# Order of the key and value projections in a four-layer Perceiver kernel, and the number of projection pieces issued per stage

## The chip, the core and the metric

The kernel runs as one program on one core of a Trainium2 chip. The metric is device time in microseconds (us) of one execution; the time of a kernel is the median of its runs. Engines are named as the profile names them: PE is TensorE (PEld its weight loads), DVE is VectorE, ACT is ScalarE, POOL is GpSimd, SP is SyncE. DMA transfers are issued by SP, ACT and POOL and carried out by 16 DMA engines.

## What is computed

The state x has 128 rows of 256 numbers. Four layers follow each other, and each has a cross attention over a context of 12,544 rows of 256 numbers, a self attention and a feed-forward part:

```python
x = x + L0_xattn(layernorm(x), ctx, mask, ...)     # l0x
x = x + L0_attn(layernorm(x), ...)                 # l0a
x = x + L0_ffn(layernorm(x), ...)                  # l0f: 16 experts
x = x + L1_xattn(ctx, ctx, layernorm(x), fside_SxS2, fside_BxS2, ...)   # l1x
x = x + L1_attn(layernorm(x), ...)                 # l1a
x = x + L1_ffn(layernorm(x), ...)                  # l1f: 8 experts
x = x + L2_xattn(layernorm(x), ctx, ctx, ...)      # l2x
x = x + L2_attn(layernorm(x), ...)                 # l2a
x = x + L2_ffn(layernorm(x), ...)                  # l2f: piecewise linear GELU
x = x + L3_xattn(layernorm(x), ctx, ctx, mask, ...)   # l3x
x = x + L3_attn(layernorm(x), ...)                 # l3a
x = x + L3_ffn(layernorm(x), ...)                  # l3f: 8 experts
```

A cross attention has 16 heads of 16 numbers:

```python
q = split_heads(x @ Wq + bq)
k = split_heads(ctx @ Wk + bk)      # 12,544 keys
v = split_heads(ctx @ Wv + bv)
logits = einsum('bhqd,bhkd->bhqk', q, k) / 4 + mask terms
out = einsum('bhqk,bhkd->bhqd', softmax(logits), v)
```

l1x also adds a 128 x 12,544 table to the logits. All data is 32-bit. The keys and values of all four layers depend on the context alone, and on nothing that an earlier layer computes.

## The kernel before

**Projection pieces.** `projections` (line 181) makes for each layer a list of jobs, here called pieces, and appends all four lists to one queue, `self.jobs`. The context is cut into 25 chunks c of 512 rows (the last has 256). A piece does one of four things with one chunk: "K" projects the first eight heads' keys, "k" the other eight heads' keys, "V" and "W" the values of the chunk's first and second 256 rows. A layer has 99 pieces. The string of a *pass* gives the order: with `"KkVW"`, each chunk's four pieces follow each other, chunk by chunk; `["KVW", "k"]` goes through all chunks with K, V, W and then through all chunks again with k. Each pass loads every chunk once.

- A key piece (`keys`, line 224) is one PSUM bank of PE work (128x512, two contraction halves). ACT copies the result with its bias into the first half of a staging tile "kst", DVE writes the rounding remainder into its second half (line 231), and two DMAs of 256 KB, issued by POOL (line 236), write the halves to DRAM. "kst" has two buffers.
- A value piece (`values`, line 245) is one bank of PE work, and ACT copies it into a staging tile `vst`, of which there are two. After the second of a chunk (or the only one of the last) POOL issues one DMA of 544 KB (line 265).
- The chunk itself, 512 KB, is loaded by SP (line 216) into one of three buffers. The first piece of each chunk in a pass asks for the loads of this chunk and the next two (of the first two only, for the first piece of a layer). The layer's projection weights are loaded by POOL (line 211) along with its first chunk; each layer's `load` knows only its own chunks.

**When pieces run.** Pieces are taken from the front of the queue in three ways. `pump(n)` takes n. `need(keys)` takes pieces until the named ones are done. And outside the cross attentions every call of `one` (a PSUM bank for a step of l0a, l0f, ...) first takes one piece, so that a piece stands between two steps of these stages on PE; l2f also pumps once for each of its 16 kinks (line 1218).

**A cross attention** (`cross`, line 383) goes through *ticks* in an order written out by hand; PE, ACT, DVE, POOL and SP each follow the order in which the program issues to them. A tick covers up to 2048 keys in four strips of 512 for one head. In tick n, PE computes the scores of tick n, and DVE takes their maximum per query ("first"). `lag` ticks later the scores are computed again, transposed and with the maximum subtracted ("second"), ACT takes the exponential, and PE multiplies with the values. l0x, l2x and l3x have 104 ticks and a lag of 15; l1x works on groups of four heads and has 100 ticks and a lag of 27. So the first `lag` ticks have only score work, the last `lag` only the second half. At tick n SP is told to load the key tiles of tick n+2 (`load_first`, 256 KB) and the value tiles of the second part two ticks ahead (`load_second`). Before the key tiles of a block of 2048 keys are loaded, `need` makes sure that the K or k pieces of this block and the next are done; for the values, the same with V and W.

**Numbers of pieces.** At each tick `cross` pumps as many pieces as `counts` (line 1410) says for its layer. By these rules and the passes, 100 pieces run up to the end of l0x (all 99 of l0x, one of l1x), 57 in l0a and l0f, 121 in l1x, 69 in l1a and l1f, 15 in l2x, 29 in l2a and l2f, 5 in l3x.

**Other tiles** named below: `l0x_c`, `l1x_c`, ... are context chunks; `l1x_ks` is l1x's staged key tile and `l1x_kx` its place in DRAM; `vst` and `l1x_vx` the same for values; `l1x_kw` are key projection weights; `l0x_s`, `l0x_t` are the first and second scores (and `l0x_s<-l0x_kx` the key tile's load); `l1x_f`, `l1x_g` are tiles of l1x's added table.

Of the kernel before, what the change touches and what calls it, by code (L numbers as in the profile page):

```python
# [70 lines left out]
def _block(b):  # L71

    return (4, SEG) if b < NB - 1 else (2, P)
# [8 lines left out]
def r32(ap):  # L82

    return ap.bitcast(F32R)
# [10 lines left out]
class Net:  # L95
# [84 lines left out]

    def projections(self, names):
        self.kx, self.vx = {}, {}
        for l, name in enumerate(CROSS):
            if name not in names:
                continue
            gw = 17 * GROUP[name]
            for b in range(NB):
                ns, seg = _block(b)
                self.kx[name, b] = self.dp.tile([16, 32 * ns, seg], F32, name=f"{name}_kx{b}",
                                                tag=f"{name}_kx{b}")  # L190
                self.vx[name, b] = self.dp.tile([272 // gw, P, ns * seg // P, gw], F32,
                                                name=f"{name}_vx{b}", tag=f"{name}_vx{b}")
            if l == 0:
                passes = ["KVW", "k"]
            else:
                passes = ["KkVW"]
            self.project(name, passes)

    def project(self, name, passes):

        nc = self.nc
        order = [(p, c) for p in passes for c in range(NCH)]
        ctx, held = {}, {}

        def load(n):
            if n >= len(order) or n in ctx:
                return
            if n == 0:
                for kv, half in (("k", 0), ("v", 512)):
                    w = self.bp.tile([P, 512], F32, name=f"{name}_{kv}w", tag=f"{kv}w")  # L210
                    nc.gpsimd.dma_start(out=w, in_=self.io[f"w_{name}_kv"][:, half : half + 512])
                    held[kv] = w.rearrange("p (c f) -> p c f", c=2)
            c = order[n][1]
            m = min(SEG, S2 - c * SEG)
            t = self.bp.tile([P, 2, SEG], F32, name=f"{name}_c{n}", tag="ctx", bufs=3)
            nc.sync.dma_start(out=t[:, :, :m],
                              in_=self.io["ctxT"][:, c * SEG : c * SEG + m]
                              .rearrange("(c p) k -> p c k", p=P))
            ctx[n] = t

        def keys(n, half, c):
            m = min(SEG, S2 - c * SEG)
            b, t = c // 4, c % 4
            ns, seg = _block(b)
            k = self.bp.tile([P, 2, SEG], F32, name=f"{name}_ks{half}_{c}", tag="kst")
            ps = self.bank(f"{name}_k{half}_{c}")
            self.mm(ps[:, :m], [held["k"][:, i, half * P : (half + 1) * P] for i in range(2)],
                    [ctx[n][:, i, :m] for i in range(2)])
            kb = self.col(f"{name}_kb")[:, half : half + 1]
            nc.scalar.activation(r32(k[:, 0, :m]), ps[:, :m], AF.Identity, bias=kb)  # L230
            nc.vector.scalar_tensor_tensor(out=r32(k[:, 1, :m]), in0=ps[:, :m], scalar=kb,
                                           in1=k[:, 0, :m], op0=ALU.add, op1=ALU.subtract)
            for at in range(0, m, seg):
                r = 32 * (t + at // seg)
                for i in range(2):
                    nc.gpsimd.dma_start(
                        out=self.kx[name, b][8 * half : 8 * half + 8,
                                             r + 16 * i : r + 16 * i + 16, :],
                        in_=k[:, i, at : at + seg])

        def values(n, part, c):
            G = GROUP[name]
            b = c // 4
            if part == 0:
                held["vs"] = self.vst[self.nvst % 2]
                self.nvst += 1
            v = held["vs"].rearrange("p (g h) a e -> p g a h e", h=G)
            vf = held["vs"].rearrange("p h a e -> p (h a e)").rearrange(
                "p (g a h e) -> p g (a h) e", g=16 // G, a=4, h=G)
            ps = self.bank(f"{name}_v{c}_{part}")  # L250
            for i in range(2):
                at = (2 * part + i) * P
                self.mm(ps.rearrange("p (g i f) -> p g i f", g=16 // G, i=2)[:, :, i, :],
                        [ctx[n][:, j, at : at + P] for j in range(2)],
                        [held["v"][:, j, :].rearrange("p (g f) -> p g f", g=16 // G)
                         for j in range(2)])
            nc.scalar.copy(vf[:, :, 2 * part * G : (2 * part + 2) * G, 0:16],
                           ps.rearrange("p (g j e) -> p g j e", g=16 // G, e=16))
            last = c == NCH - 1
            if part == 1 or last:  # L260
                m = 2 if last else 4
                flat = held["vs"].rearrange("p h a e -> p (h a e)").rearrange(
                    "p (g f) -> p g f", g=16 // G)
                at = 4 * (c % 4)
                nc.gpsimd.dma_start(
                    out=self.vx[name, b][:, :, at : at + m, :].rearrange("g p a e -> p g (a e)"),
                    in_=flat[:, :, : m * 17 * G])

        for n, (parts, c) in enumerate(order):
            for kind in parts:  # L270
                if kind == "W" and c == NCH - 1:
                    continue

                def job(n=n, c=c, kind=kind, first=kind == parts[0]):
                    if first:
                        for i in range(3 if n else 2):
                            load(n + i)
                    if kind in "Kk":
                        keys(n, int(kind == "k"), c)
                    else:  # L280
                        values(n, int(kind == "W"), c)
                self.jobs.append(((name, kind, c), job))
# [100 lines left out]
    def cross(self, name, side=False, project=True, quota=None):  # L383
# [6 lines left out]
        with ExitStack() as es:  # L390
# [307 lines left out]
            lag = per + LEAD  # L698
            pending = None
            load_queries(0)  # L700
            with tc.manual_schedule():
                qs[0] = queries(0)
                for n in range(len(ticks) + lag):
                    load_first(n + 2)
                    if n >= lag - 2:
                        load_second(n - lag + 2)
                    new = scores(n if n < len(ticks) else None, n - lag if n >= lag else None)
                    if n < len(ticks) and n % per == per - 1:
                        lower(n // per)
                    if n >= per and n % per == 0 and n // per <= 16 // G:  # L710
                        spread(n // per - 1)
                    if n % per == per // 3 and n // per + 1 < 16 // G:
                        load_queries(n // per + 1)
                    if n % per == 2 * per // 3 and n // per + 1 < 16 // G:
                        qs[n // per + 1] = queries(n // per + 1)
                    self.pump(quota(n, len(ticks), lag))
                    if n >= lag:
                        if pending:
                            values(pending)
                        if n > lag + 1 and (n - lag - 1) % per == 0:  # L720
                            finish((n - lag - 1) // per - 1)
                        pending = new
                values(pending)
                finish(16 // G - 1)
# [457 lines left out]
    def l2_ffn(self):  # L1182

        nc = self.nc
        with self.tc.tile_pool(name="l2f", bufs=1) as pool, \
# [27 lines left out]
            for i, (at, c) in enumerate(_gelu_kinks()):  # L1213
                t = a
                if i:
                    t = rp.tile([P, 1024], F32, name=f"l2f_k{i}", tag="k")
                    nc.scalar.activation(t, a, AF.Relu, bias=self.const("kinks")[:, i : i + 1])
                self.pump(1)
                nc.vector.scalar_tensor_tensor(out=y, in0=t, scalar=c, in1=y, op0=ALU.mult,
                                               op1=ALU.add)  # L1220
            nc.vector.tensor_scalar(out=h, in0=h, scalar1=0.0, scalar2=None, op0=ALU.max)
# [178 lines left out]
    def run(self, steps):  # L1400
# [4 lines left out]
        for i in range(8):  # L1405
# [2 lines left out]
        self.masks(names)  # L1408
        self.projections(names)
        counts = {  # L1410
            "l0x": lambda n, m, lag: int(n % 3 > 0) if 14 <= n < 54 else 0,
            "l1x": lambda n, m, lag: int(n % 4 != 3),
            "l2x": lambda n, m, lag: int(n < lag),
            "l3x": lambda n, m, lag: int(n < lag),
        }
# [196 lines left out]
```

## Time and profile before

| | us |
|---|---|
| median of 3 runs | 2657.65 (2648.64 to 2659.61) |
| the profiled execution | 2661.88 |
| its span, first to last instruction | 2660.1 |

| stage, by the timeline | from | to | us |
|---|---|---|---|
| start to l0x's first maximum | 0 | 96 | 96 |
| l0x, from the first maximum to the last exponential | 96 | 586 | 490 |
| l0a, l0f, start of l1x | 586 | 773 | 187 |
| l1x, ticks 0 to 26 (scores only) | 773 | 942 | 169 |
| l1x, rest | 942 | 1470 | 528 |
| l1a, l1f, start of l2x | 1470 | 1721 | 251 |
| l2x | 1721 | 2085 | 364 |
| l2a, l2f, start of l3x | 2085 | 2195 | 110 |
| l3x | 2195 | 2553 | 358 |
| l3a, l3f | 2553 | 2660 | 107 |

Within l0x, the first maximum of tick 8 is at 185, of tick 22 at 236, of tick 27 at 259, of tick 53 at 380 and of tick 54 at 394.

The page's first part gives the share of the span in which each engine was busy; the second part cuts the span into 40 slices of 66.5 us and shows tenths:

```profile
PE 2412.7 (91%) x41075; PEld 1874.3 (70%) x41075; DVE 1719.1 (65%) x3814; ACT 1229.3 (46%) x2256; POOL 419.6 (16%) x803
...
PE   7789989999968799999999898799999949999969
...
PEclk9889999999978889989899999899999967999979
DMA  8887774418967798877778676674343563444315
```

PE is busy for 91% of the span. The slices in which it is not (the first two, 12 to 14, 25, 32) are the start, the beginning of l1x, l1f and l2f. In the instructions' views a line gives start, duration, engine, line of the kernel, operation, tiles (what is written `<-` what is read), shapes, and in brackets how long the engine had been idle before it and what ended that wait.

### The profile page before, as it was taken

The page shows a single profiled execution, that of the slowest core. Times are in us where ns is not written, and L with a number is a line of the kernel's source. Part 1 is how long each engine was busy: PE and PEld are TensorE (multiplying, and loading weights), DVE is VectorE, ACT ScalarE, POOL GpSimd, SP SyncE. Part 2 cuts the span into 40 slices and gives each one's busy share as a digit, 9 for nine tenths or more (in the row PEclk, how much of TensorE's full clock was granted, in tenths as well). Part 3 has the DMA queues.
Part 4 walks back from the last instruction along what each step waited for, and adds up shares of the span by engine and source line. Part 5 has one row for each costly group of instructions (what it writes and reads, how often), then busy time and mean ns, then how long its engine had stood idle before and what let it go on. Part 6 is the DMA issues. An engine that isn't in the chain of part 4 may idle for free. (4 is left out here: it accounts for less than half of the span.)

```text
span 2660.1 us, 94232 instructions
## 1 busy us (share of the span) xinstructions
PE 2412.7 (91%) x41075; PEld 1874.3 (70%) x41075; DVE 1719.1 (65%) x3814; ACT 1229.3 (46%) x2256; POOL 419.6 (16%) x803
## 2 busy tenths in 40 slices
PE   7789989999968799999999898799999949999969
PEld 5567668886745577677677665478888737888858
DVE  1247668834134599989887753398887358888731
ACT  2225546663312145444457334446666532666642
POOL 3321110003322311111111332210000221000001
PEclk9889999999978889989899999899999967999979
DMA  8887774418967798877778676674343563444315
GB/s 277 246 260 216 226 215 135 134 53 287 296 195 215 232 323 276 298 251 256 274 246 274 188 205 196 198 238 137 115 137 95 155 193 100 136 119 135 102 49 208
DMA packets 256707, 524.56 MB, mean 197 GB/s; under 512 B 55692, under 2 KB 71510, under 8 KB 252326
## 3 DMA queue, kind: packets, MB, share of 16 engines
q1 hardware_dynamic: 175488, 309.75, 35.1%
q0 software_dynamic: 79312, 206.56, 26.6%
q8 instruction: 323, 5.29, 0.8%
q10 hardware_dynamic: 1494, 2.23, 0.2%
q14 instruction: 90, 0.74, 0.1%
HBM read 360.41 MB, written 157.79 MB: 195 GB/s over the span
## 5 line engine op out<-in xcount | busy, mean ns | idle before, releaser
L585 ACT ACTIVATE l1x_e<-l1x_e 128x512 f32<-128x512 f32 x392 | 234.0, 632 | 243.8 <-DVE l1x_e L579 243.8
L562 DVE CUSTOM_DVE_ANT_0 l1x_j<-l1x_s,l1x_f 128x512 f32<-128x512 f32 (+1 forms) x416 | 254.3, 655 | 55.3 <-DMA l1x_f<-in_fside 28.6
L567 DVE TENSOR_REDUCE l3x_mxs<-l3x_s 128x1 f32<-128x512 f32 (+1 forms) x400 | 244.1, 673 | 58.3 <-PE l3x_s L613 58.2
L567 DVE TENSOR_REDUCE l2x_mxs<-l2x_s 128x1 f32<-128x512 f32 (+1 forms) x400 | 249.2, 675 | 43.1 <-PE l2x_s L613 37.3
L567 DVE TENSOR_REDUCE l0x_mxs<-l0x_s 128x1 f32<-128x512 f32 (+1 forms) x400 | 244.3, 673 | 49.4 <-PE l0x_s L613 49.1
L585 ACT ACTIVATE l0x_e<-l0x_t 128x512 f32<-128x512 f32 (+1 forms) x400 | 203.9, 593 | 127.5 <-PE l0x_t L613 122.7
L585 ACT ACTIVATE l3x_e<-l3x_t 128x512 f32<-128x512 f32 (+1 forms) x400 | 203.8, 593 | 114.0 <-PE l3x_t L613 110.2
L585 ACT ACTIVATE l2x_e<-l2x_t 128x512 f32<-128x512 f32 (+1 forms) x400 | 203.5, 594 | 112.9 <-PE l2x_t L613 112.9
L579 DVE TENSOR_TENSOR l1x_e<-l1x_t,l1x_g 128x512 f32<-128x512 f32 x392 | 243.3, 683 | 11.2 <-PE l1x_t L613 10.0
L613 PE MATMUL l1x_t<-l1x_q,l1x_t 32*128 32x128 f32 x3136 | 174.0, 268 | 3.9 <-DMA l1x_t<-l1x_kx 3.6
L613 PE MATMUL l3x_t<-l3x_q,l3x_s 32*128 32x128 f32 x3136 | 171.3, 260 | 0.0
L613 PE MATMUL l0x_t<-l0x_q,l0x_s 32*128 32x128 f32 x3136 | 168.5, 259 | 3.0 <-issue 3.0
L613 PE MATMUL l2x_t<-l2x_q,l2x_s 32*128 32x128 f32 x3136 | 165.2, 262 | 0.0
L613 PEld LDWEIGHTS l3x_t<-l3x_q,l3x_s 32*128 32x128 f32 x3136 | 164.0, 189 | 0.0
L613 PE MATMUL l1x_s<-l1x_mrow,l1x_cq 32*128 32x256 f32 (+1 forms) x800 | 136.1, 333 | 30.1 <-DVE l1x_mxs L562 14.7
L613 PEld LDWEIGHTS l0x_t<-l0x_q,l0x_s 32*128 32x128 f32 x3136 | 161.0, 186 | 3.3 <-issue 3.3
L613 PEld LDWEIGHTS l1x_t<-l1x_q,l1x_t 32*128 32x128 f32 x3136 | 157.5, 190 | 6.9 <-DMA l1x_t<-l1x_kx 6.8
L613 PE MATMUL l1x_s<-l1x_s,l1x_q 32*128 32x256 f32 (+1 forms) x1600 | 150.8, 298 | 6.1 <-DMA l1x_s<-l1x_kx 5.9
L613 PE MATMUL l0x_s<-l0x_s,l0x_q 32*128 32x256 f32 (+1 forms) x1600 | 149.9, 289 | 6.2 <-DMA l0x_s<-l0x_kx 6.2
L613 PE MATMUL l2x_s<-l2x_s,l2x_q 32*128 32x256 f32 (+1 forms) x1600 | 150.4, 308 | 3.8 <-DMA l2x_s<-l2x_kx 3.5
L613 PEld LDWEIGHTS l2x_t<-l2x_q,l2x_s 32*128 32x128 f32 x3136 | 153.5, 186 | 0.0
L613 PE MATMUL l3x_s<-l3x_s,l3x_q 32*128 32x256 f32 (+1 forms) x1600 | 152.1, 289 | 0.2 <-issue 0.2
(668 smaller groups left out, 5788.0 us busy)
## 6 DMA issues: line engine op xcount, KB each, us to landing
l0x_c<-in_ctxT SPq DMA_DIRECT2D x48, 512.0 KB
l0x_kx<-l0x_ks POOLq DMA_DIRECT2D x96, 256.0 KB, 7.8
l0x_s<-l0x_kx SPq DMA_DIRECT2D x96, 256.0 KB
l1x_kx<-l1x_ks POOLq DMA_DIRECT2D x96, 256.0 KB, 6.7
l1x_s<-l1x_kx SPq DMA_DIRECT2D x96, 256.0 KB
l1x_f<-in_fside SPq DMA_DIRECT2D x96, 256.0 KB
l2x_kx<-l2x_ks POOLq DMA_DIRECT2D x96, 256.0 KB, 6.2
l1x_t<-l1x_kx SPq DMA_DIRECT2D x96, 256.0 KB
```

Source lines behind the costliest of these rows:

```text
L562: nc.vector.tensor_tensor_reduce(out=junk[:, :seg], in0=bank[:, j * seg : (j + 1) * seg], in1=ft[g, b][t][:, :seg], scale=1.0, scalar=-3.0e38,
L567: nc.vector.tensor_reduce(out=out, in_=bank[:, : len(hs) * seg].rearrange("p (h k) -> p h k", h=len(hs)), axis=AX.X, op=ALU.max)
L579: nc.vector.tensor_tensor(out=e[:, t, :m].rearrange("p (h q) -> p h q", h=G), in0=src.rearrange("p (h q) -> p h q", h=G), in1=ft["t", g, b ...
L585: nc.scalar.activation(e[:, t, :m], src, AF.Exp)
L613: nc.tensor.matmul(out, lhs, rhs, start=start, stop=stop, skip_group_check=True)
```

## The change

The queue's order and the numbers of pieces change; what each piece does does not.

- l0x's passes become "K" and then "VWk": the first eight heads' keys of all chunks come first, then chunk by chunk the values and the other keys. l1x and l3x get two passes, "Kk" and "VW": all keys, then all values, with each chunk loaded twice. l2x stays with "KkVW".
- The loads of all layers form one list, `self.loads`, and the first piece of a chunk issues loads up to two further on in this list, also across the end of a layer.
- In `cross`, the loads for the second part are issued ahead of those for the first part of the same tick.
- l2f pumps at every third kink, six times instead of 16.
- `counts` has other numbers for l0x and l1x.

With this, 114 pieces run up to the end of l0x (its own 99 by tick 21, and 15 keys of l1x in ticks 22 to 26), 57 in l0a and l0f (35 keys, then 22 value pieces), 123 in l1x (40 in ticks 0 to 26, where there were 46), 69 in l1a and l1f (3 of l2x, then all 50 keys of l3x, then 16 value pieces), 15 in l2x, 18 in l2a and l2f, none in l3x.

```diff
     def projections(self, names):
         self.kx, self.vx = {}, {}
+        self.loads, self.fetched = [], 0
...
             if l == 0:
-                passes = ["KVW", "k"]
+                passes = ["K", "VWk"]
             else:
-                passes = ["KkVW"]
+                passes = ["KkVW"] if name == "l2x" else ["Kk", "VW"]
             self.project(name, passes)
...
         ctx, held = {}, {}
+        base = len(self.loads)
 
         def load(n):
-            if n >= len(order) or n in ctx:
-                return
             if n == 0:
...
         for n, (parts, c) in enumerate(order):
+            self.loads.append(lambda n=n: load(n))
             for kind in parts:
...
                     if first:
-                        for i in range(3 if n else 2):
-                            load(n + i)
+                        while self.fetched < min(len(self.loads), base + n + 3):
+                            self.loads[self.fetched]()
+                            self.fetched += 1
...
                 for n in range(len(ticks) + lag):
-                    load_first(n + 2)
                     if n >= lag - 2:
                         load_second(n - lag + 2)
+                    load_first(n + 2)
...
-                self.pump(1)
+                if i % 3 == 0:
+                    self.pump(1)
...
-            "l0x": lambda n, m, lag: int(n % 3 > 0) if 14 <= n < 54 else 0,
-            "l1x": lambda n, m, lag: int(n % 4 != 3),
+            "l0x": lambda n, m, lag: 0 if n < 10 else 2 if n < lag else 3 if n < 27 else 0,
+            "l1x": lambda n, m, lag: 1 + n % 2 if n < lag else int(n % 6 > 0),
             "l2x": lambda n, m, lag: int(n < lag),
             "l3x": lambda n, m, lag: int(n < lag),
```

## The prediction

> **What bounds the kernel now.** I read the engines' busy time over stretches first, then the timelines of PE and ACT, then the DMA issues. "Piece" is one pump job: a key piece (K; k for the second half) or half a value pair (V, W).
>
> ```profile
> 32.00:82.00 50.00, 45.61 (x165) 31.64 (x163) 5.75 (x8) 13.14 (x23) 17.60 (x26) 0.97 0.97 280
> 642.00:740.00 98.00, 92.57 (x430) 70.08 (x429) 19.71 (x36) 31.24 (x56) 34.66 (x55) 0.97 0.93 313
> 821.00:890.00 69.00, 57.79 (x312) 37.65 (x311) 23.62 (x58) 15.35 (x25) 20.78 (x33) 0.89 0.80 235
> 1505.00:1575.00 70.00, 69.89 (x373) 52.91 (x372) 52.35 (x137) 24.18 (x40) 26.06 (x40) 1.00 0.73 206
> ```
>
> Columns: stretch, us, busy PE, PEld, DVE, ACT, POOL, granted PE clock, DMA share, GB/s. PE is nearly full everywhere, but at the start and in l0f the DMA engines are full too (0.97, 0.93).
>
> ```profile
> 21.43 1.88 PE L343 MATMUL l0x_k<-l0x_c,l0x_kw 128*128 128x512 f32 x4
> 23.15 3.62 PE L343 MATMUL l0x_v<-l0x_vw,l0x_c 128*128 128x256 f32 x16
> 26.60 1.88 PE L343 MATMUL l0x_k<-l0x_c,l0x_kw 128*128 128x512 f32 x4
> ```
>
> A piece costs PE 1.72 to 1.73 us, whatever its kind (start to start: 23.15-21.43, and (26.60-23.15)/2).
>
> ```profile
> 864.87 0.69 ACT L230 ACTIVATE l1x_ks<-l1x_k,cols 128x512 fp32r<-128x512 f32 x1 [2.24 <-DMA l1x_kx<-l1x_ks]
> 869.48 0.69 ACT L230 ACTIVATE l1x_ks<-l1x_k,cols 128x512 fp32r<-128x512 f32 x1 [3.93 <-DMA l1x_kx<-l1x_ks]
> ...
> 874.67 0.69 ACT L230 ACTIVATE l1x_ks<-l1x_k,cols 128x512 fp32r<-128x512 f32 x1 [3.54 <-DMA l1x_kx<-l1x_ks]
> 879.37 0.69 ACT L230 ACTIVATE l1x_ks<-l1x_k,cols 128x512 fp32r<-128x512 f32 x1 [4.01 <-DMA l1x_kx<-l1x_ks]
> ...
> 882.81 0.69 ACT L230 ACTIVATE l1x_ks<-l1x_k,cols 128x512 fp32r<-128x512 f32 x1 [1.79 <-DMA l1x_kx<-l1x_ks]
> ```
>
> This forced burst in l1x shows what a key piece costs beyond PE. The staging tile "kst" has two buffers, so ACT's copy of a key piece waits until the two write-backs of the key piece two before have landed: one key piece per (882.81-864.87)/4 = 4.49 us. All five copies were released by a landing, none by PE. Two copies under a lighter DMA load, and two in l1a:
>
> ```profile
> 2153.84 0.69 ACT L230 ACTIVATE l3x_ks<-l3x_k,cols 128x512 fp32r<-128x512 f32 x1 [1.56 <-DMA l3x_kx<-l3x_ks]
> ...
> 2156.89 0.69 ACT L230 ACTIVATE l3x_ks<-l3x_k,cols 128x512 fp32r<-128x512 f32 x1 [0.29 <-DMA l3x_kx<-l3x_ks]
> 1563.57 0.69 ACT L230 ACTIVATE l3x_ks<-l3x_k,cols 128x512 fp32r<-128x512 f32 x1 [1.08 <-PE l3x_k L343]
> 1566.17 0.69 ACT L230 ACTIVATE l3x_ks<-l3x_k,cols 128x512 fp32r<-128x512 f32 x1 [1.92 <-PE l3x_k L343]
> ```
>
> The copies two before 2153.84 and 2156.89 began at 2146.92 and 2149.62: 7.1 us for two, 3.55 a piece. In l1a pieces come every 2.60 us in the order K, k, V, W, and PE releases the copy: the values between two pairs hide the write-back.
>
> ```profile
> l0x_kx<-l0x_ks POOLq DMA_DIRECT2D x96, 256.0 KB, 7.8
> ...
> l1x_kx<-l1x_ks POOLq DMA_DIRECT2D x96, 256.0 KB, 6.7
> ...
> l3x_kx<-l3x_ks POOLq DMA_DIRECT2D x96, 256.0 KB, 5.4
> ```
>
> The last number is issue to landing. With ACT 0.69, a wake-up and two issues of 0.60 on POOL, some 1.6 us, the loop is (1.6+5.4)/2 = 3.5 us a key piece by l3x's row, 4.15 by l1x's, 4.7 by l0x's.
>
> **The change, part by part.** It removes no computation; it moves pieces. Its passes put key pieces in runs: 25 in l0x, then l1x's 15 in l0x's ticks 22-26 and 35 in l0a/l0f, then 50 of l3x (behind 2 of l2x) in l1a/l1f. Queued behind a waiting copy on ACT are l0x's exps, l0f's ReLUs and l1a's copies, so PE waits too. I call the pitch in a run p, and take 4.2 for l0x's run (1.05 MB each, load and write-back: at 280 GB/s no less than 3.75), 3.8 in ticks 22-26, 4.3 in l0f (0.79 MB and a third of an expert's 0.79 MB: 1.05 MB, 3.35 at 313 GB/s), 3.5 in l1a. Bounds for all: 2.6, the spacing where nothing waits, and 6.0, half of the 12 us that two key pieces take in the first 96 us.
>
> *l0x.* First copy at 28.9 as now; 25 x 4.2 = 105: tick 7 ends near 136 (now tick 8 begins at 185, a gain of about 45). Ticks 8-10: 6. Then the 74 V, W, k pieces by tick 21. PE: 74 x 1.73 + 7 full ticks x 3.2 + 5 score-only ticks x 1.0 (877.42 to 878.41 in PE's timeline) = 155. DMA: about 39 MB and 12 ticks' tiles of 0.54 MB, 45.5 MB at 280 GB/s = 162. I take 163, to 305; now tick 22 begins at 236. The 15 keys: 15 x 3.8 = 57, to 362 (now tick 27: 259). Ticks 27-53 without pieces: 27 x 3.2 = 86, to 448; now tick 54 begins at 394. So **+54**. One real saving is inside:
>
> ```profile
> 387.48 3.75 PE L343 MATMUL l1x_k<-l1x_c,l1x_kw 128*128 128x512 f32 x4 [6.69 <-DMA l1x_kw<-in_w_l1x_kv]
> ```
>
> l1x's weights are issued only when its first piece runs, and PE idles 6.7 us. The shared list of loads issues them two pieces ahead, past two pieces' write-backs on POOL (4 x 0.60 us).
>
> *l0a, l0f.* 57 pieces now at 2.95 (copies from 589.0 to 754.3); then 35 x 4.3 + 22 values x 2.61 = 208 against 168: **+40**.
>
> *l1x.* 40 pieces in ticks 0-26 instead of 46, none forced: 40 x 1.73 + 27 x 2.76 of score matmuls + 9 for queries and start = 153 against 169, -16. Later 8 pieces more x 1.73 = +14. **-2**. Value and feature tiles are now issued ahead of the key tiles on SP: between all 28.6 us of DVE's waits for l1x_f won and as much lost; SP runs ticks ahead, so 0.
>
> *l1a, l1f.* Some 28 keys fall where the pitch is 2.6: 28 x 0.9 = +25; 16 values in l1f at 3.3 instead of 3.6: -5. **+20**.
>
> *l2x, l2a/l2f, l3x.* 15 value pieces without DVE's 0.75: -1. l2f: its 16 kinks take 32.6 (2125.5 to 2158.1 in the timeline); with 6 value pieces DVE's 16 x 1.23 and ACT's 15 x 1.14 + 6 x 0.59 leave 22.5: -10, l2a -2. l3x starts without its 5 pieces: -5. **-18**.
>
> l1x and l3x load the context twice: 25.7 MB, 92 us at 280 GB/s if nothing hid it. Beside PE work in l1x it is hidden; where the engines are full it is in p.
>
> The sum: +54+40-2+20-18 = **+94**. The profiled span is 2660.1 (its run 2661.88, 4.2 above the median); on the median 2657.65 that is **2752 us**.
>
> A rule that speaks for the change: the Trainium skill, "DMA: Bandwidth & Descriptors", section "Anatomy of one DMA — SWDGE (gpsimd) path", fits a GpSimd-issued DMA as about 2.0 us plus bytes at 436 GB/s, an estimated 2.6 us for 256 KB. By it the loop would be some 2.1 us a piece, no copy would wait, and the time would be that of the first rival; the landings above are two to three times as long.
>
> One that speaks against: "TensorE: Matmul & The Clock Gate", section "HAM oscillation — how this bites in real kernels", has the clock drop when PE pauses over about 3.4 us. The row here: 0.89 where PE is busy 57.79 of 69. Even at half clock a key piece (3.4 us) lies under p, so I add nothing.
>
> **Rivals.** *Write-backs return in time* (faster). Without values' write-backs beside them, two landings fit in 5.2 us; the place is l0f, the DMA must reach its best slice at the start, 386 GB/s: l0x's run at 1.05/0.386 = 2.7 gives l0x 28.9+68+6+157+42+86+192 = 580, -6; l0f -19; l1a 0-5; the rest -20: **2608**. For: the landings near 4 us where little else moves. Against: the copies above, and 10.4 to 13.8 us for two wherever a landing released one in l0f. It decides where p averages under 3.05.
>
> *A wash*: 103 keys (25+15+35+28) carry the loss, at a mean p of 3.99, so the time is about 2752 - 103 x (3.99 - p); at p = 3.05 to 3.15 the savings in l2f, l3x and at the layer switch cancel it: **2660**. *Saturation*: p stays near 5.3, as at the start: l0x +102, l0f +75, l1a +70, rest -20: **2885**.
>
> **How the numbers follow.** Forecast 0.70, write-backs in time 0.14, wash 0.10, saturation 0.06. The likeliest's own range is 2700-2804 (p within 0.5: 103 x 0.5 = 52); to hold 8 in 10 I reach to 2645 and 2835. A run can tell about 0.5% from no change: faster 0.14, same 0.10, slower 0.76.
>
> **What would show it.** Right: in l0f ACT's key copies released by "DMA l1x_kx" nearly every time, 8 to 9 us for two; tick 8 of l0x near 140 but tick 27 near 360; l0a/l0f some 225 us long; l2a/l2f near 98. Wrong: copies in runs released by PE; l0x ending before 600.

## The result and the profile after

The changed kernel is slower: 2823.82 us (median of 4 runs, 2812.99 to 2828.8) against 2654.54 for the kernel before in the same comparison, a ratio of 1.0633 [1.0589, 1.0677]. Its profiled execution took 2812.99 us with a span of 2811.2, so between the two profiles lie 151 us of the 169 between the medians; the stages below are those of the profiles. A cross attention begins with DVE's first maximum and ends with ACT's last exponential.

| stage | before, us | after, us | difference | predicted |
|---|---|---|---|---|
| start to the end of l0x | 586.0 | 670.5 | +84.5 | +54 |
| l0a, l0f | 187.5 | 230.3 | +43 | +40 |
| l1x, ticks 0 to 26 | 166.9 | 123.6 | -43 | -16 |
| l1x, the rest | 529.9 | 547.5 | +17.5 | +14 |
| l1a, l1f | 250.5 | 310.8 | +60 | +20 |
| l2x to the end | 939.3 | 928.5 | -11 | -18 |

First the busy time over stretches of the changed kernel, with the columns of before: the start, l0f, the early ticks of l1x, l1a.

```profile
32.00:82.00 50.00, 17.76 (x52) 7.13 (x50) 8.17 (x11) 7.45 (x11) 13.18 (x22) 0.68 0.75 217
690.00:788.00 98.00, 68.17 (x229) 38.59 (x229) 35.49 (x55) 24.63 (x40) 30.48 (x52) 0.86 0.78 235
901.00:1026.00 125.00, 111.68 (x998) 82.95 (x1000) 76.07 (x243) 25.87 (x42) 23.05 (x34) 0.94 0.89 306
1640.00:1710.00 70.00, 55.38 (x234) 33.13 (x236) 44.05 (x105) 15.54 (x25) 21.89 (x37) 0.94 0.76 209
```

In the runs of key pieces no engine is full. At the start PE is busy 17.76 of 50 us (45.61 before), and the DMA engines are busy 0.75 of the time, where they were at 0.97. In l0f it is 68 of 98 us and 0.78 (92.57 and 0.93 before). Something that is latency, not work, sets the pace there. ACT's timeline in l0f shows it:

```profile
724.50 0.69 ACT L230 ACTIVATE l1x_ks<-l1x_k,cols 128x512 fp32r<-128x512 f32 x1 [5.50 <-DMA l1x_kx<-l1x_ks]
726.54 0.69 ACT L230 ACTIVATE l1x_ks<-l1x_k,cols 128x512 fp32r<-128x512 f32 x1 [1.35 <-DMA l1x_kx<-l1x_ks]
727.12 0.47 ACT L834 ACTIVATE l0f_t<-l0f_h,row_l0f_b 128x256 f32<-128x256 f32 x1
...
734.64 0.69 ACT L230 ACTIVATE l1x_ks<-l1x_k,cols 128x512 fp32r<-128x512 f32 x1 [5.32 <-DMA l1x_kx<-l1x_ks]
736.29 0.69 ACT L230 ACTIVATE l1x_ks<-l1x_k,cols 128x512 fp32r<-128x512 f32 x1 [0.96 <-DMA l1x_kx<-l1x_ks]
736.88 0.47 ACT L834 ACTIVATE l0f_t<-l0f_h,row_l0f_b 128x256 f32<-128x256 f32 x1
```

Each key copy is released by the landing of a key piece's write-back; the copies two apart are 734.64-724.50 = 10.1 and 736.29-726.54 = 9.8 us apart. l0f's own ReLUs (line 834) wait their turn behind them. In l0a and l0f 30 of the 35 key copies were released so. Over the whole kernel, 32 key copies with 82 us of idle time before them were released in this way in the kernel before, and 89 with 322 us after. In l0x's ticks 22 to 26, where exponentials stand behind the copy, it is 6 of 15; the others waited for PE, mostly for its next piece:

```profile
343.83 0.69 ACT L230 ACTIVATE l1x_ks<-l1x_k,cols 128x512 fp32r<-128x512 f32 x1 [7.65 <-DMA l1x_kx<-l1x_ks]
344.42 1.08 ACT L587 ACTIVATE l0x_e<-l0x_t 128x512 f32<-128x512 f32 x2
...
350.89 0.69 ACT L230 ACTIVATE l1x_ks<-l1x_k,cols 128x512 fp32r<-128x512 f32 x1 [2.78 <-PE l1x_k L345]
...
360.14 0.69 ACT L230 ACTIVATE l1x_ks<-l1x_k,cols 128x512 fp32r<-128x512 f32 x1 [6.85 <-DMA l1x_kx<-l1x_ks]
360.73 2.05 ACT L587 ACTIVATE l0x_e<-l0x_t 128x512 f32<-128x512 f32 x4
```

On the profile's page, the group of l0x's score matmuls shows how this reaches PE, and the DMA issues give the landings (last number: issue to landing in us):

```profile
L615 PE MATMUL l0x_s<-l0x_mrow,l0x_cq 32*128 32x256 f32 (+1 forms) x800 | 135.3, 326 | 48.1 <-DVE l0x_ks L231 36.8
l0x_kx<-l0x_ks POOLq DMA_DIRECT2D x96, 256.0 KB, 6.8
l1x_kx<-l1x_ks POOLq DMA_DIRECT2D x96, 256.0 KB, 6.2
```

PE waited 36.8 us for DVE's second half of a key tile (line 231), all of it in l0x's first eight ticks. DVE computes it from ACT's copy, and only then does the PSUM bank come free for the scores: the wait for a DMA goes through ACT and DVE to PE. The landings are even a little shorter than before (7.8 and 6.7; these are medians over the whole kernel, and in the runs themselves they are 5.4 to 6.2); what changed is how often somebody waits for one.

### The profile page after: what moved, and what is told of

Its sections match the earlier page's. It is cut to its first block, busy times and chain, and to the rows that moved or that the text cites. A ratio compares the mean times of both kernels' runs of the same rounds, so it can differ in the third digit from the quotient of the medians.

```text
span 2811.2 us, 94247 instructions
## 1 busy us (share of the span) xinstructions
PE 2435.8 (87%) x41075; PEld 1874.9 (67%) x41075; DVE 1725.2 (61%) x3814; ACT 1228.7 (44%) x2256; POOL 413.4 (15%) x803
## 4 chain that ended last, share of the span: by engine, by line
PE 22%; issue 20%; DMA 4%; DVE 3%; POOL 3%; ACT 2%; POOLq 0%; SPq 0%; ACTq 0%; DVEq 0%
PE l2x_t L615 5%; PE l2x_av L666 3%; PE l2x_s L615 2%; PE l3x_v L345 2%; POOL l3x_kx L236 2%; PE l1x_t L615 2%; PE l1x_av L666 1%; PE l2x_k L345 1%; ACT l2x_e L587 1%; PE l2x_v L345 1%; DVE l3x_mxs L569 1%; DMA l1x_s<-l1x_kx 1%; PE l1x_s L615 1%; DVE l2f_y L1222 1%; DMA l3x_vx<-vst 0%
## 5 line engine op out<-in xcount | busy, mean ns | idle before, releaser
L615 PE MATMUL l0x_s<-l0x_mrow,l0x_cq 32*128 32x256 f32 (+1 forms) x800 | 135.3, 326 | 48.1 <-DVE l0x_ks L231 36.8
L615 PE MATMUL l3x_s<-l3x_mrow,l3x_cq 32*128 32x256 f32 (+1 forms) x800 | 144.6, 334 | 21.7 <-DMA l3x_mrow<-l3x_row 19.9
```

Of the source, the lines that this page charges most:

```text
L615: nc.tensor.matmul(out, lhs, rhs, start=start, stop=stop, skip_group_check=True)
```

## The experiments

Ratios are against the kernel before, run on the same chip in the same comparison; its median there was 2661 to 2664 us (2654.54 for the row "after"). Differences in us between rows of different comparisons are therefore good to some 10 us. The next table has the stages of each profiled execution in us (l1x in its two parts).

| run | edit | l0x end | l0a, l0f | l1x | l1a, l1f | l2x on | ratio |
|---|---|---|---|---|---|---|---|
| before | | 586 | 188 | 167+530 | 251 | 939 | |
| after | | 671 | 230 | 124+548 | 311 | 929 | 1.0633 [1.0589, 1.0677] |
| e1_kst3 | kst 3, room from f and junk | 622 | 213 | 133+583 | 263 | 928 | 1.0357 [1.0308, 1.0407] |
| e2_kst4 | kst 4, two key tiles fewer too | 620 | 191 | 130+599 | 256 | 930 | 1.0232 [1.0188, 1.0276] |
| e5_cut | the cuts of e1 alone | 676 | 233 | 137+584 | 314 | 931 | one run: 2874 us |
| e6_kst3b | kst 3, room from junk | 621 | 212 | 120+556 | 263 | 929 | 1.0169 [1.0138, 1.0200] |
| e3_l13 | l1x's, l3x's passes undone | 644 | 186 | 131+551 | 246 | 933 | 1.0105 [1.0064, 1.0145] |
| e4_l0 | l0x's passes and numbers undone | 569 | 264 | 116+549 | 305 | 928 | 1.0295 [1.0243, 1.0347] |
| e7_kkvw | both undone | 584 | 180 | 171+556 | 247 | 929 | 1.0045 [1.0017, 1.0072] |
| e8_kvkw | e7, order K, V, k, W | 578 | 175 | 173+544 | 247 | 936 | 0.9978 [0.9955, 1.0000] |
| e9_before_kst3 | before with kst 3 | 583 | 177 | 173+530 | 256 | 936 | 0.9977 [0.9953, 1.0001] |
| e10_l1counts | e7, l1x's numbers undone | 579 | 179 | 168+544 | 252 | 937 | 1.0017 [0.9990, 1.0044] |
| e11_best | e8, e9, e10 together | 577 | 175 | 170+545 | 257 | 935 | 0.9987 [0.9962, 1.0013] |
| e12_best_order | e11, loads ordered as before | 576 | 178 | 163+539 | 256 | 937 | 0.9942 [0.9916, 0.9968] |

### More buffers for the staged keys

Theory: the loop "copy, issue, landing" over two buffers. Rival: the DMA engines are full, and more buffers bring nothing.

```diff
-            k = self.bp.tile([P, 2, SEG], F32, name=f"{name}_ks{half}_{c}", tag="kst")
+            k = self.bp.tile([P, 2, SEG], F32, name=f"{name}_ks{half}_{c}", tag="kst", bufs=3)
```

For the room, `e1_kst3` and `e5_cut` give junk one buffer and f five (`bufs=1`, `bufs=5`); `e2_kst4` has `bufs=4` here, the same cuts, and 12 key tiles in l1x instead of 14; `e6_kst3b` drops junk and lets DVE write over the score bank it reads:

```diff
-                                out=junk[:, :seg], in0=bank[:, j * seg : (j + 1) * seg],
+                                out=bank[:, j * seg : (j + 1) * seg],
+                                in0=bank[:, j * seg : (j + 1) * seg],
```

> The changed kernel with a third buffer of the staging tile kst; to make room in l1x, the tile junk has one buffer instead of two and the feature tile f five instead of six. Theory (the two-buffer loop: copy, issue, landing of the write-back): the loop over three buffers would give two thirds of the measured pitches, 3.05, 3.3, 2.85 and 2.55 us per key piece instead of 4.58 (l0x's run), 4.95 (ticks 22 to 26), 4.26 (l0f) and 3.8 (l1a); the bytes put a floor of 3.75, 3.75 and 3.35 under the first three, so 24 x 0.8 + 14 x 1.2 + 34 x 0.9 + about 45 x 1.0 = 110 us less, 2700 us or a ratio near 1.02. Rival (the DMA engines are full in those stretches, and a landing takes as long as it does because of that): the landings get longer by half, the pitches stay, and the time is within 15 us of the changed kernel's 2824 (ratio 1.058 to 1.064). Control of the cuts: DVE's waits for l1x_f in l1x, 28.6 us before the change, should not grow by more than 10 us.

> The changed kernel with four buffers of kst; besides the cuts of the run with three, l1x has 12 key tiles instead of 14. Theory (loop): half of the measured pitches is below the floors of the bytes everywhere, so against three buffers little more is won, 0 to 20 us: 2680 to 2700. Rival (full DMA engines): as with three buffers, within 15 us of 2824. If three buffers win and the fourth loses, the two key tiles fewer in l1x cost time: then l1x itself is longer and not the runs.

> The changed kernel with the cuts of the run with three buffers alone: junk one buffer, feature tile f five, kst two as in the changed kernel. Reading of the run with three buffers: what it lost in l1x after tick 26 (583 us against 547) came from the five feature tiles. Then this kernel is 30 to 45 us longer than the changed one, 2840 to 2860, all of it in l1x, with DVE's waits for l1x_f near 47 us instead of 32, and key pieces in l0x and l0f at the pitch of the changed kernel (4.6 and 4.3). Rival (the third staging buffer lets l1x's own pieces collide with its loads): l1x is 540 to 550 us after tick 26 as in the changed kernel, total within 10 us of 2824.

> The changed kernel with three buffers of kst and all six feature tiles; the room comes from junk, whose values DVE now writes over the score bank in PSUM that it reads. If the five feature tiles cost l1x its 35 us, this is 2755 - 35 = 2720, ratio 1.022, with l1x near 545 us after tick 26. If the third buffer itself disturbs l1x, or DVE's write to PSUM is slower, it stays at 2745 to 2760.

Three buffers took 69 us off the changed kernel's 2823.82 in e1 (2754.68), and four took 102 off (2721.75). Both fall short of the theory's 2700 and 2680 to 2700, because l1x got longer: by 44 us in e1's profile and by 58 in e2's. DVE's waits for l1x_f grew to 47.0 us in e1, more than the expectation allowed. The cuts alone (e5) cost l1x's later ticks 36 us, as much as e1 lost there, but l1x's early ticks 13 us too, and the one run took 2874.45, above the expected 2840 to 2860. Without those cuts (e6) the third buffer gives 2707.47: 1.0633 becomes 1.0169, 116 us or so less, at l0x's end 50 us, in l0a and l0f 18, in l1a and l1f 48. That is better than the expected 2720, though l1x's later ticks stayed at 556 us instead of 545; each of DVE's 416 maxima there took 684 ns on the mean, where it took 655 with junk. The rival falls, and the stretches of e6 say why (start, l0f, l1a):

```profile
32.00:82.00 50.00, 23.09 (x115) 9.87 (x114) 16.18 (x24) 10.78 (x16) 18.08 (x31) 0.80 0.89 273
660.00:758.00 98.00, 74.42 (x272) 45.85 (x271) 32.90 (x42) 23.50 (x42) 35.38 (x60) 0.88 0.90 280
...
1560.00:1630.00 70.00, 64.32 (x283) 38.33 (x282) 52.34 (x121) 20.26 (x31) 29.21 (x49) 0.99 0.93 273
```

The DMA engines go from 0.75, 0.78 and 0.76 to 0.89, 0.90 and 0.93, and move 273 to 280 GB/s instead of 209 to 235: they had room that two buffers could not use. The pitch of the key copies falls from 4.58 to 3.28 us in l0x's run and from 4.95 to 3.56 in ticks 22 to 26. Two thirds would be 3.05 and 3.30; the landings stretch, and not every copy of these runs waits for a landing. e6's rows are

```profile
l0x_kx<-l0x_ks POOLq DMA_DIRECT2D x96, 256.0 KB, 8.0
l1x_kx<-l1x_ks POOLq DMA_DIRECT2D x96, 256.0 KB, 7.5
```

against 6.8 and 6.2 with two buffers, and 8.5 and 8.7 with four. Here the rival comes into its own: with the DMA engines near 0.9, a landing takes longer.

### The passes undone, layer by layer

```diff
 e3_l13
-                passes = ["KkVW"] if name == "l2x" else ["Kk", "VW"]
+                passes = ["KkVW"]
 e4_l0
-                passes = ["K", "VWk"]
+                passes = ["KVW", "k"]
...
-            "l0x": lambda n, m, lag: 0 if n < 10 else 2 if n < lag else 3 if n < 27 else 0,
+            "l0x": lambda n, m, lag: int(n % 3 > 0) if 14 <= n < 54 else 0,
```

> The changed kernel with the passes of l1x and l3x as before (K, k, V, W of a chunk together, the context loaded once); l0x's passes, the numbers of pieces and the shared loads stay changed. Theory (runs of key pieces): the stage l0a/l0f loses its +43 and l1a/l1f its +60 against the kernel before, ticks 22 to 26 of l0x (15 mixed pieces, half of them values) take 45 to 55 us instead of 76; the early ticks of l1x lose some 20 of the 43 they had won, because values stand ahead of needed keys again. 2824 - 43 - 60 - 25 + 20 = 2716, ratio 1.023. Rival (the numbers of pieces per stage make the loss, not the order): l0f and l1a/l1f stay long, 2800 or more.

> The changed kernel with l0x's passes (keys and values of a chunk together, second keys last) and its numbers of pieces as before; l1x's and l3x's passes and the rest stay changed. Theory (runs of key pieces): l0x ends near 590 instead of 670, with l1x's first key pieces spread two in three ticks over its later ticks, too far apart to wait; l0a/l0f keeps its loss (230 us long against 187 before) and l1a/l1f too (311 against 250): 2824 - 84 = 2740, ratio 1.032. Rival (l0x lost its time to the 15 pieces of l1x that were moved into it, work that is saved elsewhere): l0x wins its 84 us back but l0f and the early ticks of l1x are longer by 40 or more, and the time is 2780 or above.

The theory held in e3, and in e4 for the total. With mixed pieces in l1x and l3x (e3), l0a and l0f fall to 186 us, l1a and l1f to 246, and ticks 22 to 26 of l0x from 76 to 47 us with the same number of pieces; the time is 2686.38, 30 us better than expected. Early l1x lost 7 us and not 20, which makes 13 of the 30; the rest is that the changed kernel's profile lies 11 us under its median and e3's 6 over. In e3, PE releases ACT's copies in l0f, two keys and two values in turn:

```profile
685.15 0.69 ACT L230 ACTIVATE l1x_ks<-l1x_k,cols 128x512 fp32r<-128x512 f32 x1 [1.25 <-PE l1x_k L345]
687.76 0.69 ACT L230 ACTIVATE l1x_ks<-l1x_k,cols 128x512 fp32r<-128x512 f32 x1 [1.25 <-PE l1x_k L345]
690.35 0.59 ACT L257 COPY vst<-l1x_v 128x512 f32<-128x512 f32 x1 [1.90 <-PE l1x_v L345]
```

One piece per 2.6 us, keys and values alike. With l0x's part undone (e4), l0x ends at 569 instead of 671, 17 us ahead of the kernel before; l0a and l0f are longer still (264), as 49 key pieces now fall into the run there instead of 35. The time is 2737.81, expected 2740, but that is luck: l0x ended 21 us earlier than expected (590), and l0a and l0f took 34 longer (230).

### Everything but the passes

`e7_kkvw` has both edits above. `e10_l1counts` takes back l1x's numbers too:

```diff
-            "l1x": lambda n, m, lag: 1 + n % 2 if n < lag else int(n % 6 > 0),
+            "l1x": lambda n, m, lag: int(n % 4 != 3),
```

> All passes as before, and l0x's numbers of pieces as before; what stays of the change: l1x's numbers of pieces, the shared list of loads, the loads' order in a tick, six pieces in l2f instead of 16. Theory (the order of the passes makes the loss, the rest of the change is a small gain): l0x 569 as in the run with l0x's part undone (-17 against before, the stall at the switch to l1x's weights and some more), l0a/l0f as before, l1x within 10, l1a/l1f -4, l2f -8, l3x -3: 2661 - 30 = 2630, ratio 0.988. Rival (l0x gained only because values were put off that l0f and l1x have to make up): ratio 0.997 to 1.01.

> As the kernel with all passes and l0x's numbers undone, and l1x's numbers of pieces as before too; what stays of the change: the shared loads, the order of the loads in a tick, six pieces in l2f. l1x after tick 26 was 556 us there and 530 before, with 68 key pieces against 62 in l1x. If the numbers of pieces made that, l1x is 530 to 535 here, and with l2f's 8 and l0x's few us kept the time is 2640 to 2650, ratio 0.992 to 0.996. If the order of the loads made it (value and feature tiles ahead of key tiles on SP; DVE's waits for l1x_f 40 us against 29), l1x stays near 555 and the ratio is 1.00 to 1.005.

e7 missed the 2630 us that I expected: 2677.56, a ratio of 1.0045, still inside the interval that its rival named. So the passes, with l0x's numbers of pieces, make the ratio's fall from 1.0633 to 1.0045, some 146 us, and the rest of the change is no gain. The passes of l1x and l3x alone (e3) took it to 1.0105; l0x's passes and its numbers were only ever undone together, so their shares are not known apart. The small savings are there (l0x 2 us, l0a and l0f 8, l2x on 10), but l1x took 26 more in its later ticks. With l1x's numbers undone (e10) it is 544 there: 12 of the 26 went. The ratio 1.0017 is that of the second expectation (the order of the loads), but l1x's 544 lies between the two, and the time can't be told from no change.

### Is the wait the order's own?

`e9_before_kst3` is the kernel before with e6's two edits; `e8_kvkw` is e7 with `passes = ["KVkW"]`.

> The kernel before with three buffers of kst, junk in place of the score bank as in the run of the changed kernel with six feature tiles. Theory (the order of the change only made a wait frequent that the kernel before already had): in the kernel before ACT's key copies wait 47 us for landings in the first 96 us, 19 us in l0f, 33 us in the forced stretches of l1x; a third buffer takes away some two thirds where the DMA engines are not full: 20 + 12 + 20 = 50 us less, 2612, ratio 0.981. Rival (with values between the keys the waits of ACT lie beside other waits, for loads and PE): ratio 0.995 to 1.0. In any case it says how much of the 116 us that the third buffer gave the changed kernel is the order's own.

> As the kernel with all passes undone, but the pieces of a chunk in l1x, l2x and l3x in the order K, V, k, W, so that a value piece stands between every two key pieces. Theory (a key piece waits only if the one two before is less than a round trip, some 8 us, behind it): pairs K, k already hide it at a spacing of 2.6 us in l1a, but where landings take 10 us (l0f) the even spacing helps: 5 to 15 us less than with K, k, V, W, in l0f and the forced stretch of l1x. Rival (nothing waits in the mixed order): within 5 us of it. A forced stretch can also get longer by a value piece per chunk, 3 us each.

The third buffer, worth some 116 us to the changed kernel, is worth 6 to the kernel before (2657.04 against 2662.94, an interval that reaches 1). I had expected 50, and the rival's ratio held: ACT's waits for landings did fall there (from 25 us to none in the first 96 us, from 19 to none in l0a and l0f, from 33 to 15 in early l1x), but little time came out. The expectation's 47 us for the first 96 had counted ACT's first wait in, 22 us, which no write-back's landing ended. In the profiles l0a and l0f are 11 us shorter, early l1x and l1a, l1f 6 and 5 longer; ACT's waits for PE grew in l0a and l0f (from 33 to 44 us before key copies), and e6's slower maxima are in e9 too (680 ns), so how much they hide is not shown. So the buffer is no gain of that size by itself; nearly all of it repairs what the order does. K, V, k, W was 19 us faster than K, k, V, W, but not by the mechanism that I gave: up to tick 26 of l1x 32 key copies were still released by a landing, 85 us of idle time in all, where e7 had 30 and 78. In the profiles 12 us of the gain lie in l1x's later ticks, where no key copy waited for a landing in either. Why it is faster is open.

### The good parts together

`e11_best` is e8 with l1x's numbers as before and with e6's edits. `e12_best_order` is e11 with one edit:

```diff
-                    if n >= lag - 2:
-                        load_second(n - lag + 2)
                     load_first(n + 2)
+                    if n >= lag - 2:
+                        load_second(n - lag + 2)
```

> The parts that looked good together: K, V, k, W within a chunk for l1x, l2x and l3x, l0x as before, three buffers of kst, l1x's numbers of pieces as before, the shared loads and six pieces in l2f. If the parts add up: the run with K, V, k, W (2659), less 13 for l1x's numbers, less 50 for the third buffer: near 2596, ratio 0.975. If the third buffer brings nothing once values stand between the keys: 2645, ratio 0.993.

> The run of the good parts together, with one edit: the loads of a tick in the order of the kernel before, key and feature tiles ahead of value tiles. With l1x's numbers of pieces as before, l1x after tick 26 was 544 and 545 us in two kernels with the changed order, 530 in two with the order before. If the order of the loads makes these 15 us, l1x after tick 26 is 528 to 533 here and DVE's waits for l1x_f fall from 41 to about 30 us; the time is 2660 - 15 = 2645, ratio 0.993. If the shared loads make them, or the spread between kernels, l1x stays near 545 and the ratio is 0.997 to 1.001.

The parts do not add up: e11 took 2660.04 against 2662.94, though 2596 or 2645 were expected. With the loads in the order of before (e12) it is 2650.00 against 2663.43, ratio 0.9942 [0.9916, 0.9968]: the only version here whose interval lies wholly below 1, by 0.6%, or 0.3 to 0.8. Later l1x took 539 us, between the 530 and 545 that the two readings asked for, and DVE's waits for l1x_f stayed (43 us, 41 in e11). So the order of the loads is not shown as the cause; l1x's 10 to 15 us stay open.

## Why the prediction was right, and where its sizes were off

Direction and mechanism were right: in l0a and l0f 30 of 35 key copies were released by landings, two copies took 9.1 us (forecast 8 to 9), the stage 230 (some 225); tick 8 began at 149 (near 140), l2a and l2f took 100.8 (98). Tick 27 began at 390, not near 360. The measured 2824 lies in the range, close to its upper end: 72 us above the forecast, and 20 above the range 2700 to 2804 that the forecast's own mechanism was given. Between the profiles the sum was +94 against +151, and it would have been further off without luck: l0x and l1a, l1f were 30 and 40 us too low, and early l1x's gain, 27 us larger than forecast, took about two fifths of that back. The terms, one by one:

- **l0x's start, +54 against +84.5.** "First copy at 28.9 as now" was wrong by 8.5 us. ACT's timeline in the kernel before, then in the changed one:

```profile
27.64 1.23 ACTq L1385 DMA_DIRECT2D l0x_mrow<-l0x_row  x4
28.92 0.69 ACT L230 ACTIVATE l0x_ks<-l0x_k,cols 128x512 fp32r<-128x512 f32 x1 [22.09 <-DMA l0x_mrow<-l0x_row]
...
31.78 5.61 ACTq L1388 DMA_DIRECT2D l0x_mrow<-l0x_row  x4
37.44 1.27 ACT L230 ACTIVATE l0x_ks<-l0x_k,cols 128x512 fp32r<-128x512 f32 x2 [30.55 <-DMA l0x_c<-in_ctxT]
```

  ACT first issues the DMAs of l0x's mask rows; the last four took it 5.61 us, in the kernel before 1.23, and the key copies stood behind them. In e4 and e7, with values between l0x's first keys, the copy came at 28.64 and 29.18 again. I had not looked at what was ahead of the first copy on ACT. Then p was 4.58, not 4.2: 24 x 0.38 = 9 us. It was 4.06 for the twelve copies ahead of the first maximum, and 5.03 for the thirteen from there on: ticks 0 to 7 stand between these pieces on PE, and the forecast had no term for them.
- **Ticks 22 to 26, "15 x 3.8 = 57".** They took 76 us, the largest single miss in l0x. The pitch was 4.95, but not for slow landings: these took 5.4 us there (median), so that the forecast's loop would give 3.5. Only 6 of the 15 copies were released by a landing. Three pieces are taken per tick, PE stands still behind the copy that waits, and only then does the tick's own work follow. The step took the five ticks' work as hidden; at the forecast's own 3.2 us a tick it is 16 us, and 57 + 16 = 73. That this sum is the cause was not tested by itself. With values among the pieces (e3) the five ticks take 47, with the third buffer (e6) 54. Ticks 8 to 21 took 165 (6 + 163 = 169 forecast) and 27 to 53 88 (86).
- **l0a and l0f, +40 against +43.** Right, and nearly by its own steps: 34 gaps at 4.56 us (4.3 forecast, 9 us less), then values every 2.61; two of these ran beside the last keys.
- **l1x's early ticks, -16 against -43.** The 40 pieces were right. The step "27 x 2.76 of score matmuls" was mis-sized: the score matmuls kept PE busy 33.5 us in these ticks, 1.24 each; 2.76 is what four maxima of 0.69 take on DVE, beside PE. The kernel before had it in view: 40.9 us in the same 27 ticks, and the forecast itself read 1.0 us for such a tick. With 1.24 the sum is 69 + 33.5 + 9 = 112, which is what PE shows busy (111.68 of 125).
- **l1x's later ticks, +14 against +17.5.** Near, but perhaps for the wrong reason: in e7, with the passes undone, it is +26, of which l1x's numbers of pieces make 12 and something still open the rest.
- **l1a and l1f, +20 against +60.** "28 x 0.9" was the worst term. 52 key copies fell there instead of 36; in l1a they came at some 4.0 us (31 copies from 1608.88 to 1728.39), not 3.5, and in l1f they waited too, which I had left out. Of 47 pieces between 1608 and 1815, 29 were key copies released by a landing. The third buffer takes 48 of the 60 us back, the undone passes 65.
- **l2x to the end, -18 against -11.** Right in kind: l2a and l2f -10 (forecast -12), l3x -3 (-5); the last two stages 2 longer.

Of the rivals, *write-backs return in time* (2608) fell. The Trainium skill, "DMA: Bandwidth & Descriptors", section "Anatomy of one DMA — SWDGE (gpsimd) path", would have had a 256 KB write-back land after an estimated 2.6 us; the medians here are 5.4 (l3x) to 8.7 (l1x with four buffers), longer the more of them were under way, and the measurement decides. *Saturation* (2885) came as near in time as the forecast (61 us above the result, the forecast 72 below), but its mechanism is not what bound the changed kernel: the DMA engines stood at 0.75 in the run, and filled only when a third buffer let them. That it is what remains in e6, 44 us above the kernel before with pitches of 3.3 to 3.9 us and a DMA share near 0.9, fits the second load of the context (25.7 MB more), but no run tested that by itself.

The clock was rightly left out. It stood at 0.68 at the start (0.97 before) and 0.917 on the whole (0.937), low where PE waits: e6, where PE is busy for 23.09 of the same 50 us instead of 17.76, has it at 0.80 there. Even a piece that is longer by 1/0.68, an estimated 1.73 / 0.68 = 2.5 us, is shorter than the pitch of 4.58.

## What to carry to other kernels

Work that leaves through a staging tile has a pace of its own: at best the round trip of one buffer divided by the number of buffers. Grouping such work makes that pace everybody's pace, because an in-order engine that waits at the tile holds back all that is queued behind it; spreading it among work of another kind hid most of the same round trip here (l0a and l0f took 186 us in e3 and 230 grouped). When you price such a run, ask not only how long the round trip is but what stands between two pieces on the engines that wait: here the landings in the runs were as short as forecast or shorter, and much of what the forecast missed in l0x lies where whole ticks stood between pieces. And add a buffer with the grouping or not at all: with the mixed order it brought nothing that could be told from zero.

## What was not expected of the hardware

- The time from issue to landing of a 256 KB write-back (l1x's, median) follows the number that can be under way: 6.2 to 7.1 us in the kernels with two staging buffers, 7.4 to 8.0 with three, 8.7 with four.
- Cutting the feature tiles of l1x from six to five (and junk from two to one) cost its later ticks 36 us; DVE's waits for l1x_f came in 27 places instead of 13, though their sum grew only from 32.0 to 39.9 us.
- DVE writing its elementwise result over the PSUM bank that it reads, instead of into junk, made each of l1x's 416 maxima longer: 655 ns on the mean in the kernel before, 680 in e9, 684 in e6, some 11 us of DVE's time in all. The stage did not show it: later l1x took 530 us in the kernel before and in e9, though e9 has the third buffer too.
